# A four-layer perceiver in f32: norms tile by tile at the stage borders of its first layer, and small steps moved to GpSimd

## The chip, the cores and the metric

The kernel runs on one core of a Trainium2 chip. The metric is the device time in microseconds (us) of one execution, the median of the runs. A profile of one execution gives the trace from which all other durations are taken. The engines are named as in the profile: PE is TensorE's matmul, PEld its weight load, DVE is VectorE, ACT is ScalarE, POOL is GpSimd and SP is SyncE, which issues the DMAs. L12 is line 12 of the kernel.

## The reference

The network updates a residual stream x of 8 x 64 tokens by 256 channels. It reads a context of 1601 keys by 128 channels for each of the 8 batches. Each of its four layers has an attention into the context, a self-attention and a feed-forward part. The change touches the first layer, and a few bias rows and biases in the later ones. Its core is this (cut):

```python
def _mha(x, y, wq, wk, wv, li1_w, li1_b, lnx_g, lnx_b, lny_g, lny_b, ln3_g, ln3_b, li2_w, li2_b, li3_w, li3_b, causal):
    xn = _ln(x, lnx_g, lnx_b)
    yn = _ln(y, lny_g, lny_b)
    ...
    x_out = x + o @ li1_w + li1_b
    h = jax.nn.gelu(_ln(x_out, ln3_g, ln3_b) @ li2_w + li2_b, approximate=False)
    return x_out + h @ li3_w + li3_b
...
# xx is ln1(x); the second attention reads the context
# xx = ln2(xx + a1(xx, xx)); xx = a2(xx, context)
x = x + _L0_xattn_ref(_layernorm(x, axis=-1), ctx_512, ...)
x = x + _L0_attn_ref(_layernorm(x, axis=-1), ...)
x = x + _L0_ffn_ref(_layernorm(x, axis=-1), ...)
```

The comment lines put the body of the first attention block in words: a causal self-attention a1 with its own MLP, a norm with a gain and a bias (ln2), and a cross-attention a2 with its own MLP. b0 is the self-attention with rotated queries and keys that follows, and f0 the mixture of experts after it.

## The kernel before

The 512 tokens are held as four tiles (NI = 4) of 128 tokens by 256 channels in X, a tensor of 128 partitions x 4 x 256. The context has 13 tiles of keys (KT = 13). The stages run one after the other: a1, its MLP, a2, its MLP, b0, f0, and then three more layers (x1, r1, f1; x2, b2, f2; x3, b3, f3). Each engine works through its own queue in the order in which the kernel was scheduled, and pools of buffers decide when a tile may be written.

A norm of one tile (`normed_tile`, L324 to L333) takes five instructions. DVE computes the statistics (L328), the mean and variance (L330) and adds epsilon (L331). POOL raises the variance to the power of minus one half (L332, "the pow"). DVE subtracts the mean and multiplies (L333). `normed` does this for four tiles. `transposed` (L345) turns the normed tensor with PE through the identity (L352), and DVE copies the answer out with the gain and bias of the norm (L357), 512 columns at a time. `lin_T` (L363) then multiplies so that the channels lie on partitions ("psl" in the profile), and `lin_nat` (L373) so that the tokens do ("psn"); `lin_nat` hands each tile of its answer to a function `done`. `add_to` builds such a function: it adds the answer to one operand (L386) and then to further ones (L388) on DVE.

`after_attention` (L1092) is the MLP of a1 and of a2: norm, transposition, `lin_T` to 1024 channels with the gelu on ACT (L1101), `lin_nat` back to 256, where the answer and the row of biases are added to xo.

Four borders matter in what follows.

- Border 1, from a1 to its MLP: a1's answers are added to xo tile by tile (L1139). Then come the loads of the first two batches of the context ("cn"), its statistics on DVE (L1154, L1155), its scales on POOL (L1159 to L1162) and its normalisation on ACT (L1167). Only then is `after_attention` called.
- Border 2, from that MLP to a2: x1 += o over all four tiles at once (L1178), a norm, the gain (L1180) and bias (L1181) of ln2 over all tiles, a second norm, transposition, and `lin_T` for a2's queries ("psl_q" below is this `lin_T`).
- Border 3a, from a2's attention to its MLP: the last answer ("pso", L1223) is copied to qT, `lin_nat` projects it, and `add_to` adds x1 and a row, tile by tile.
- Border 3b, from that MLP to b0: x1 += o and X += x1 over all tiles (L1253, L1254). Then `small_attention` makes the turned biases ("shift", L1270 and L1271), and b0 starts with its norms, transposes (L411) and projections ("psq", "psk", L428).

```python
fetch(0)
fetch(1)
for k in range(0, KT, 3):
    stats(0, k)
scales(0)
for k in range(0, KT, 4):
    normalise(0, k)
```

`add_row_to_X` (L1089) adds a row of biases to all of X on DVE after four later stages, and b3 makes its own shift at L1273.

Of the kernel before, what the change touches and what calls it, by code (L numbers as in the profile page):

```python
# [11 lines left out]
F32 = mybir.dt.float32  # L12
# [5 lines left out]
P = 128  # L18
# [247 lines left out]
def perceiver(ctx: ExitStack, tc: tile.TileContext, d, col_at, row_at, const_at, out):  # L266
# [17 lines left out]
    ones = keep.tile([P, P], F32, tag="ones", name="ones")  # L284
    nc.gpsimd.memset(ones, 1.0)

    def K(name):
        n, w = const_at[name]
        return const[:, n : n + w]
# [32 lines left out]

    def normed_tile(dst, src):

        st = small.tile([P, 6], F32, tag="st", name="st")
        nc.vector.bn_stats(st, src)  # L328
        mv = small.tile([P, 4], F32, tag="mv", name="mv")
        nc.vector.bn_aggr(mv[:, 0:2], st)  # L330
        nc.vector.tensor_scalar(mv[:, 3:4], mv[:, 1:2], EPS, None, ALU.add)  # L331
        nc.gpsimd.tensor_tensor(mv[:, 2:3], mv[:, 3:4], mhalf[:, 0:1], ALU.pow)  # L332
        nc.vector.tensor_scalar(dst, src, mv[:, 0:1], mv[:, 2:3], ALU.subtract, ALU.mult)  # L333

    def normed(src, name="xn"):

        dst = nat.tile([P, NI, C], F32, tag="nat", name=name)
        for i in range(NI):
            normed_tile(dst[:, i, :], src[:, i, :])
        return dst  # L340

    def bc_rows(r):
        return r.unsqueeze(1).to_broadcast([P, NI, C])

    def transposed(ps, src, *affines):  # L345

        pairs = affines or (None,)
        dsts = [tpool.tile([P, C // P, NT], F32, tag="T", name="T") for _ in pairs]
        for c in range(C // P):
            t = ps.tile([P, 512], F32, tag="ps", name="pst")  # L350
            for i in range(NI):
                nc.tensor.transpose(t[:, i * P : (i + 1) * P], src[:, i, c * P : (c + 1) * P], ident)  # L352
            for dst, pair in zip(dsts, pairs):
                if pair is None:
                    evac(dst[:, c, :], t)
                else:
                    nc.vector.tensor_scalar(dst[:, c, :], t, col(pair[0], c), col(pair[1], c), ALU.mult, ALU.add)  # L357
        return dsts if affines else dsts[0]
# [727 lines left out]
        return done  # L1086

    def add_row_to_X(name):
        nc.vector.tensor_tensor(X, X, bc_rows(row(name)), ALU.add)  # L1089

    def general(n=8):
        return tc.tile_pool(name="ps", bufs=n, space=PSUM)  # L1092

    def after_attention(pre, xo, pool, ps):

        li2, li3 = chunks(weight(pre + "li2"), 1024), chunks(weight(pre + "li3"), C)
        [x3] = transposed(ps, normed(xo), (pre + "ln3_g", pre + "ln3_b"))
        hT = pool.tile([P, 8, NT], F32, tag="mlp", name="mlp")  # L1100
        lin_T(ps, li2, x3, 1024, lambda c, t: nc.scalar.activation(hT[:, c, :], t, AF.Gelu, bias=col(pre + "li2_b", c)))  # L1101
        r3 = row(pre + "li3_b")
        lin_nat(ps, li3, hT, add_to(xo, lambda i: xo[:, i, :], lambda i: r3))
        return xo

    with tc.tile_pool(name="l0res", bufs=1) as res, ExitStack() as both:
        x1 = res.tile([P, NI, C], F32, tag="x1", name="x1")
# [56 lines left out]
        def normalise(b, k):  # L1164
            mv, y = mvs[b], cns[b]
            for kt in range(k, min(k + 4, KT)):
                nc.scalar.activation(y[:, kt, :CY], y[:, kt, :CY], AF.Identity, bias=mv[:, kt, 3:4], scale=mv[:, kt, 2:3])  # L1167

        fetch(0)
        fetch(1)  # L1170
        for k in range(0, KT, 3):
            stats(0, k)
        scales(0)
        for k in range(0, KT, 4):
            normalise(0, k)
        with general() as ps, tc.tile_pool(name="m1", bufs=1) as mp:
            o = after_attention("a1", xo, mp, ps)
            nc.vector.tensor_tensor(x1, x1, o, ALU.add)  # L1178
            z = normed(x1)
            nc.vector.tensor_tensor(x1, z, bc_rows(row("ln2_g")), ALU.mult)  # L1180
            nc.vector.tensor_tensor(x1, x1, bc_rows(row("ln2_b")), ALU.add)  # L1181
        with tc.tile_pool(name="a2o", bufs=1) as op:

            qT = op.tile([P, 4, NT], F32, tag="qT", name="qT")
            with ExitStack() as _:
                wq, wk, wv, li1 = (weight("a2" + k) for k in ("wq", "wk", "wv", "li1"))
                wk3, wv3 = chunks(wk, CY), chunks(wv, P)
                with general() as ps:
                    [xT] = transposed(ps, normed(x1), ("a2lnx_g", "a2lnx_b"))
                    lin_T(ps, chunks(wq, 512), xT, 512, lambda c, t: evac(qT[:, c, :], t))  # L1190
                ps, psS, psO, fp = turned_pools("a2")
                with ps as ps, psS as psS, psO as psO, fp as fp:
                    cts, qks, oTs = {}, {}, {}
# [53 lines left out]
                    )  # L1247
                    turned_attention(ps, fp, *parts, hooks)
            with general() as ps, tc.tile_pool(name="m2", bufs=1) as mp:
                r1 = row("a2li1_b")  # L1250
                lin_nat(ps, chunks(li1, C), qT, add_to(xo, lambda i: x1[:, i, :], lambda i: r1))
                o = after_attention("a2", xo, mp, ps)
                nc.vector.tensor_tensor(x1, x1, o, ALU.add)  # L1253
                nc.vector.tensor_tensor(X, X, x1, ALU.add)  # L1254

    def small_attention(key, wq, wk, wvo, begin, xn, done, rope=None, bq=None, bk=None, bv=None):

        ps, psS, psO, pool = self_pools(key)  # L1260
        with ps as ps, psS as psS, psO as psO, pool as pool:
            shift = None
            if bq:
                shift = pool.tile([P, 4, P], F32, tag="shift", name="shift", bufs=1)
            for n, b in enumerate((bq, bk) if bq else ()):
                for c in range(2):
                    dst = shift[:, 2 * n + c, :]
                    if rope:
                        cs, sn = (x[:, c * P : (c + 1) * P] for x in rope)
                        nc.vector.tensor_scalar(dst, cs, col(b, c), None, ALU.mult)  # L1270
                        nc.vector.scalar_tensor_tensor(dst, sn, col(b + "s", c), dst, ALU.mult, ALU.add)  # L1271
                    else:
                        nc.vector.tensor_scalar(dst, ones, col(b, c), None, ALU.mult)  # L1273

            def project(i):
                [xT] = turned_tile(ps, pool, xn(i))
                if rope:
                    qk = rope_qk(ps, pool, xT, wq, wk, rope, shift)
                else:
                    t = ps.tile([P, 512], F32, tag="ps", name="psq")  # L1280
                    proj_tile(t[:, :C], wq, xT, 2)
                    proj_tile(t[:, C:], wk, xT, 2)
                    qk = pool.tile([P, 4, P], F32, tag="qkr", name="qkr")
                    nc.vector.tensor_tensor(qk, t.rearrange("p (c s) -> p c s", s=P), shift, ALU.add)
                return spread(pool, qk[:, 0:2, :], K("hm16"), 2), qk[:, 2:4, :], xT

            self_attention(ps, psS, psO, pool, begin, project, wvo[:, 0:2], wvo[:, 2:4], 16, done, bv=bv)
# [10 lines left out]
    def done0(i, t):  # L1298
# [7 lines left out]

    small_attention(
        "b0", (wq[:, 0:2], wq[:, 2:4]), (wk[:, 0:2], wk[:, 2:4]), wvo, begin0, lambda i: xn0[:, i, :], done0,
        rope=(K("r0c"), K("r0s")), bq="b0q", bk="b0k", bv="b0v",
    )  # L1310

    def attend_into_X(key, wq, wk, wvo, brow, **more):
# [350 lines left out]

    wqk, wvo = chunks(weight("b3qk"), C), chunks(weight("b3vo"), C)
    attend_into_X("b3", wqk[:, 0:2], wqk[:, 2:4], wvo, "b3d", bq="b3bq", bk="b3bk", bv="b3v")

# [45 lines left out]
```

## Time and profile before

| | before |
|---|---|
| median of 3 runs | 2319.57 us (2315.0 to 2322.26) |
| the profiled execution | 2313.45 us |
| its span | 2311.7 us |
| mean granted clock of TensorE | 0.951 |
| PE busy | 2068.4 us (89%) |
| PEld busy | 1430.7 us (62%) |
| DVE busy | 1321.3 us (57%) |
| ACT busy | 1003.3 us (43%) |
| POOL busy | 199.7 us (9%) |

The profiled execution's time is 1.75 us more than the span between its first and last record, and 6.1 us less than the median. In a line of the timeline, the first number is the start in us from the start of the span and the second the duration in us, then come the engine, the line, the operation, what it writes and reads, and how many instructions were put together; the bracket holds the idle time of the engine before it and what ended that. The granted clock is a share of full speed.

### The profile page before, as it was taken

The page shows a single profiled execution, that of the slowest core. Times are in us where ns is not written, and L with a number is a line of the kernel's source. Part 1 is how long each engine was busy: PE and PEld are TensorE (multiplying, and loading weights), DVE is VectorE, ACT ScalarE, POOL GpSimd, SP SyncE. Part 2 cuts the span into 40 slices and gives each one's busy share as a digit, 9 for nine tenths or more (in the row PEclk, how much of TensorE's full clock was granted, in tenths as well). Part 3 has the DMA queues.
Part 4 walks back from the last instruction along what each step waited for, and adds up shares of the span by engine and source line. Part 5 has one row for each costly group of instructions (what it writes and reads, how often), then busy time and mean ns, then how long its engine had stood idle before and what let it go on. Part 6 is the DMA issues. An engine that isn't in the chain of part 4 may idle for free. (4 is left out here: it accounts for less than half of the span.)

```text
span 2311.7 us, 35299 instructions
## 1 busy us (share of the span) xinstructions
PE 2068.4 (89%) x14916; PEld 1430.7 (62%) x14916; DVE 1321.3 (57%) x2171; ACT 1003.3 (43%) x1582; POOL 199.7 (9%) x258
## 2 busy tenths in 40 slices
PE   6678999999887998849999999999898899897988
PEld 5445777777675554538657777778554566565654
DVE  6346766666455223570266666675434788887533
ACT  2326766776312112301155556562114787774200
POOL 2101111110011000020000000001000111112000
PEclk9889999999988999959999999999799999999899
DMA  3210000000001225315400101001111000000010
GB/s 114 100 53 1 16 16 16 16 16 10 12 30 53 65 67 200 127 39 191 152 15 30 45 30 32 28 1 51 53 43 65 16 16 31 16 2 28 28 61 30
DMA packets 24941, 110.71 MB, mean 48 GB/s; under 512 B 3400, under 2 KB 6352, under 8 KB 21456
## 3 DMA queue, kind: packets, MB, share of 16 engines
q1 hardware_dynamic: 24784, 108.46, 13.5%
q8 instruction: 117, 1.92, 0.3%
q14 instruction: 40, 0.33, 0.0%
HBM read 107.93 MB, written 0.52 MB: 47 GB/s over the span
## 5 line engine op out<-in xcount | busy, mean ns | idle before, releaser
L837 PEld LDWEIGHTS psav<-cn,raw 128*128 128x128 f32 (+1 forms) x3328 | 402.9, 191 | 88.6 <-issue 87.3
L775 DVE TENSOR_TENSOR raw<-raw,mb 128x1024 f32<-128x1024 f32 (+1 forms) x336 | 384.0, 1147 | 84.5 <-ACT mb L771 84.5
L837 PE MATMUL psav<-cn,raw 128*128 128x129 f32 (+1 forms) x3328 | 407.0, 275 | 0.7 <-ACT raw L779 0.7
L825 PE MATMUL psS<-qk,ct 128*128 128x512 f32 (+1 forms) x832 | 397.7, 600 | 6.9 <-ACT raw L826 6.9
L753 DVE TENSOR_TENSOR top<-raw,top 128x1024 f32<-128x1024 f32 (+1 forms) x240 | 271.4, 1131 | 142.8 <-ACT raw L826 123.4
L779 ACT ACTIVATE raw<-raw 128x1024 f32<-128x1024 f32 (+1 forms) x336 | 335.4, 1001 | 15.9 <-DVE raw L775 14.9
L826 ACT COPY raw<-psS 128x512 f32<-128x512 f32 (+1 forms) x416 | 236.5, 587 | 126.4 <-PE psS L825 123.2
L825 PEld LDWEIGHTS psS<-qk,ct 128*128 128x128 f32 (+1 forms) x832 | 140.5, 187 | 129.2 <-issue 95.6
L332 POOL TENSOR_TENSOR mv<-mv,mhalf 128x1 f32<-128x1 f32 x76 | 41.6, 554 | 1130.4 <-DVE mv L331 1084.6
L1065 ACT ACTIVATE sg<-psg 128x512 f32<-128x512 f32 (+2 forms) x52 | 31.0, 596 | 244.5 <-PE psg L1062 244.4
L1066 DVE TENSOR_TENSOR hT<-sg,psu 128x512 f32<-128x512 f32 (+2 forms) x52 | 35.7, 687 | 145.4 <-PE psu L1062 145.4
L947 ACT COPY raw<-psS 128x1024 f32<-128x1024 f32 (+1 forms) x112 | 105.4, 941 | 2.0 <-PE psS L942 1.6
L942 PEld LDWEIGHTS psS<-qz,kT 32*128 32x128 f32 (+1 forms) x1664 | 54.8, 181 | 65.1 <-ACT raw L947 50.4
L747 DVE TENSOR_TENSOR top<-raw 128x1024 f32<-128x1024 f32 x48 | 58.8, 1226 | 58.8 <-ACT raw L826 36.8
L942 PE MATMUL psS<-qz,kT 32*128 32x128 f32 (+1 forms) x1664 | 76.9, 295 | 15.9 <-ACT raw L947 14.8
L963 PE MATMUL psav<-raw,v 128*32 128x128 f32 (+1 forms) x1664 | 86.7, 280 | 3.3 <-ACT raw L779 3.2
L1084 DVE SCALAR_TENSOR_TENSOR X<-psd,wt,X 128x256 f32<-128x256 f32 x128 | 58.5, 483 | 46.0 <-PE psd L1074 46.0
L963 PE MATMUL psav<-raw,ones 128*32 128x128 f32 (+1 forms) x1664 | 84.1, 274 | 0.0
L771 ACT COPY mb<-psmb 128x512 f32<-128x512 f32 x48 | 28.1, 586 | 124.9 <-PE psmb L769 124.9
L352 PE MATMUL pst<-const,xn 128*128 128x128 f32 x88 | 23.6, 384 | 54.4 <-DVE mv L331 27.7
L769 PE MATMUL psmb<-dg,ones 128*128 128x512 f32 x96 | 52.6, 630 | 13.1 <-DVE dg L763 13.0
L920 PE MATMUL psk<-ct,w_x3kv_None 128*128 128x401 f32 (+1 forms) x128 | 59.4, 550 | 0.7 <-ACT qT L319 0.7
(403 smaller groups left out, 3030.2 us busy)
## 6 DMA issues: line engine op xcount, KB each, us to landing
cn<-in_cn_dram SPq DMA_DIRECT2D x24, 838.5 KB, 4.6
ct<-in_ct_dram SPq DMA_DIRECT2D x24, 800.5 KB, 4.5
w_f1up<-in_f1up_dram SPq DMA_DIRECT2D x8, 1024.0 KB, 4.9
w_f1dn<-in_f1dn_dram SPq DMA_DIRECT2D x8, 1024.0 KB, 5.1
w_f2w<-in_f2w_dram SPq DMA_DIRECT2D x8, 768.0 KB, 4.3
w_f3w<-in_f3w_dram SPq DMA_DIRECT2D x16, 384.0 KB, 3.0
w_f0up<-in_f0up_dram SPq DMA_DIRECT2D x8, 704.0 KB, 4.0
w_f0dn<-in_f0dn_dram SPq DMA_DIRECT2D x8, 384.0 KB, 3.0
```

What stands on the lines that cost most here:

```text
L747: nc.vector.tensor_tensor(hd["top"], hd["raw", 0], raw, ALU.max)
L753: nc.vector.tensor_tensor(top[:n, :m, :], raw, top[:n, :m, :], ALU.max)
L775: nc.vector.tensor_tensor(raw, raw, halves[h]["mb"][:n].unsqueeze(1).to_broadcast([n, m, 512]), ALU.add)
L779: nc.scalar.activation(raw, raw, AF.Exp)
L825: nc.tensor.matmul(x[:n], ct[:, kt * P : kt * P + n], qk, start=True, stop=True)
L826: nc.scalar.copy(raw[:n, i, :], x[:n])
L837: nc.tensor.matmul(oa[:, j // 2, j % 2 * CO : (j % 2 + 1) * CO], w[:n, i, j * P : (j + 1) * P], cn[:n, kt, :], start=kt == 0 and j % 2 == ...
L920: nc.tensor.matmul(t[:, : hi - lo], wkv[:, c * P : (c + 1) * P], cts[b][:, lo:hi], start=True, stop=True)
L942: nc.tensor.matmul(x[:n, g, i * P : (i + 1) * P], kTs[h][r, kt * P : kt * P + n], qzs[b][r, c].rearrange("p m s -> p (m s)"), start=True, ...
L947: nc.scalar.copy(raw[:n, :m, :].rearrange("p i (g s) -> p i g s", g=4), x[:n, :, : m * P].rearrange("p g (i s) -> p i g s", s=P))
L963: nc.tensor.matmul(oa[r, at * P : (at + 1) * P], what, w[:n, i, g * P : (g + 1) * P], start=kt == 0 and at == 0, stop=kt == KT - 1 and at ...
L1084: nc.vector.scalar_tensor_tensor(X[:, i, :], t, w(i), X[:, i, :], ALU.mult, ALU.add)
```

## The change

At border 1 the norm, the transposition and the affine of each tile of xo are written as one step (`enter1` with `turn_into`), staggered by a tile against the statistics (`norm1`). A tensor `base` collects xo + x1 + the MLP's last bias row on POOL. The context's statistics, scales and normalisation, and the making of the turned biases of b0 (now on POOL, in a tensor `shift` that is kept for the whole kernel), move into `context_norm`. `after_attention` calls it between `lin_T` and `lin_nat`. At border 2, `leave1` handles each tile of the MLP's answer by itself: add, norm, gain, bias, norm, and the transposition of the tile two before it. At border 3a, POOL makes `x1r` = x1 + row and `base` = X + x1 + row, later + xo; `attended` adds and norms each tile, and the transposes run two tiles behind. At border 3b, X is the answer plus `base`, in one DVE step for each tile. `turn_into` copies the two halves of a transposed tile out by ACT and by DVE. `normed` issues the statistics of the next tile before the last step of a norm, and `transposed` goes by tiles ahead of columns. `add_row_to_X` and the shift of b3 move from DVE to POOL.

```diff
     def normed(src, name="xn"):
         dst = nat.tile([P, NI, C], F32, tag="nat", name=name)
-        for i in range(NI):
-            normed_tile(dst[:, i, :], src[:, i, :])
+        mvs = []
+        for i in range(NI + 1):
+            if i < NI:
+                mvs.append(norm_of(src[:, i, :]))
+            if i:
+                norm_by(dst[:, i - 1, :], src[:, i - 1, :], mvs[i - 1])
...
     def add_row_to_X(name):
-        nc.vector.tensor_tensor(X, X, bc_rows(row(name)), ALU.add)
+        nc.gpsimd.tensor_tensor(X, X, bc_rows(row(name)), ALU.add)
...
+    def turn_into(ps, dst, i, src, pair):
+        t = ps.tile([P, 512], F32, tag="ps", name="pst")
+        for c in range(C // P):
+            nc.tensor.transpose(t[:, c * P : (c + 1) * P], src[:, c * P : (c + 1) * P], ident)
+        for c in range(C // P):
+            d = dst[:, c, i * P : (i + 1) * P]
+            if c:
+                nc.vector.tensor_scalar(d, t[:, c * P : (c + 1) * P], col(pair[0], c), col(pair[1], c), ALU.mult, ALU.add)
+            else:
+                nc.scalar.activation(d, t[:, c * P : (c + 1) * P], AF.Identity, bias=col(pair[1], c), scale=col(pair[0], c))
...
-    def after_attention(pre, xo, pool, ps):
+    def after_attention(pre, xo, x3, pool, ps, done, meanwhile):
...
-        r3 = row(pre + "li3_b")
-        lin_nat(ps, li3, hT, add_to(xo, lambda i: xo[:, i, :], lambda i: r3))
-        return xo
+        meanwhile()
+        lin_nat(ps, li3, hT, done)
...
+        def context_norm():
+            for n, k in enumerate(("b0q", "b0k")):
+                for c in range(2):
+                    dst = shift[:, 2 * n + c, :]
+                    cs, sn = (K(x)[:, c * P : (c + 1) * P] for x in ("r0c", "r0s"))
+                    tmp = mp.tile([P, P], F32, tag="turned", name="turned", bufs=2)
+                    nc.gpsimd.tensor_scalar(tmp, sn, col(k + "s", c), None, ALU.mult)
+                    nc.gpsimd.tensor_scalar(dst, cs, col(k, c), None, ALU.mult)
+                    nc.gpsimd.tensor_tensor(dst, dst, tmp, ALU.add)
+            for k in range(0, KT, 3):
+                stats(0, k)
+            scales(0)
+            for k in range(0, KT, 4):
+                normalise(0, k)
...
+            def enter1(i):
+                norm_by(xn[:, i, :], xo[:, i, :], mvs1[i])
+                turn_into(ps, x3, i, xn[:, i, :], ("a1ln3_g", "a1ln3_b"))
+                nc.gpsimd.tensor_tensor(base[:, i, :], xo[:, i, :], x1[:, i, :], ALU.add)
+                nc.gpsimd.tensor_tensor(base[:, i, :], base[:, i, :], r3, ALU.add)
+
+            def leave1(i, t):
+                x = x1[:, i, :]
+                nc.vector.tensor_tensor(x, t, base[:, i, :], ALU.add)
+                normed_tile(z[:, i, :], x)
+                nc.vector.tensor_tensor(x, z[:, i, :], g2, ALU.mult)
+                nc.vector.tensor_tensor(x, x, b2, ALU.add)
+                normed_tile(xn[:, i, :], x)
+                turn2(i - 2)
...
+            staggered(norm1, enter1)
+            after_attention("a1", xo, x3, mp, ps, leave1, context_norm)
+            turn2(NI - 2)
+            turn2(NI - 1)
...
+                for i in range(NI):
+                    nc.gpsimd.tensor_tensor(x1r[:, i, :], x1[:, i, :], r1, ALU.add)
+                for i in range(NI):
+                    nc.gpsimd.tensor_tensor(base[:, i, :], X[:, i, :], x1[:, i, :], ALU.add)
+                    nc.gpsimd.tensor_tensor(base[:, i, :], base[:, i, :], r3, ALU.add)
+                def enter2(i):
+                    turn_into(ps, x3, i, xn[:, i, :], ("a2ln3_g", "a2ln3_b"))
+                    nc.gpsimd.tensor_tensor(base[:, i, :], base[:, i, :], xo[:, i, :], ALU.add)
+
+                def attended(i, t):
+                    nc.vector.tensor_tensor(xo[:, i, :], t, x1r[:, i, :], ALU.add)
+                    normed_tile(xn[:, i, :], xo[:, i, :])
+                    if i > 1:
+                        enter2(i - 2)
+
+                lin_nat(ps, chunks(li1, C), qT, attended)
+                enter2(NI - 2)
+                enter2(NI - 1)
+                after_attention(
+                    "a2", xo, x3, mp, ps, lambda i, t: nc.vector.tensor_tensor(X[:, i, :], t, base[:, i, :], ALU.add), lambda: None
+                )
...
+    for n, k in enumerate(("b3bq", "b3bk")):
+        for c in range(2):
+            nc.gpsimd.tensor_scalar(shift[:, 2 * n + c, :], ones, col(k, c), None, ALU.mult)
```

## The prediction, made before the changed kernel ran

> **What bounds the kernel now.** I read the page's busy line and slices first, then the table of windows around the four borders that the diff touches, then the timeline inside each border.
>
> ```profile
> PE 2068.4 (89%) x14916; PEld 1430.7 (62%) x14916; DVE 1321.3 (57%) x2171; ACT 1003.3 (43%) x1582; POOL 199.7 (9%) x258
> ```
>
> TensorE is busy for 89% of the span, so only its idle stretches can be won. They lie at the borders (columns: length, then busy us and count of PE, PEld, DVE, ACT, POOL, then the granted clock):
>
> ```profile
> 83.00:99.70 16.70, 2.56 (x8) 1.16 (x8) 7.79 (x44) 5.12 (x14) 5.42 (x8) 0.56 0.48 186
> 130.40:147.20 16.80, 2.57 (x9) 1.18 (x9) 13.50 (x45) 0.00 (x0) 4.34 (x8) 0.57 0.29 86
> 609.00:623.00 14.00, 9.28 (x57) 7.10 (x49) 8.78 (x27) 0.00 (x0) 2.41 (x4) 0.92 0.17 47
> 653.10:661.60 8.50, 0.00 (x0) 0.01 (x1) 7.96 (x24) 0.00 (x0) 2.83 (x11) 0.81 0.33 100
> 661.60:670.00 8.40, 7.88 (x38) 7.42 (x39) 3.12 (x7) 0.37 (x1) 5.25 (x8) 0.58 0.05 16
> ```
>
> PE idles 14.1, 14.2, 4.7 and 8.5 us in the first four, and the clock falls to about half. The timeline says what ends each wait:
>
> ```profile
> 87.11 0.49 DVE L1154 BATCH_NORM_STATS2 st<-cn 128x6 f32<-128x128 f32 x2 [4.36 <-DMA cn<-in_cn_dram]
> ...
> 94.49 0.56 POOL L332 TENSOR_TENSOR mv<-mv,mhalf 128x1 f32<-128x1 f32 x1
> ...
> 99.74 1.22 PE L369 MATMUL psl<-T,w_a1li_None 128*128 128x512 f32 x1 [0.69 <-DVE T L357]
> ```
>
> Border 1: DVE, in order, waits for the context's DMA, runs 13 tiles of its statistics, and only then normalises xo; POOL does the context's scales before the first pow (L332).
>
> ```profile
> 131.33 1.22 DVE L1178 TENSOR_TENSOR x<-x,xo 128x1024 f32<-128x1024 f32 x1
> ...
> 147.18 1.22 PE L369 MATMUL psl<-T,w_a2wq_None 128*128 128x512 f32 x1 [0.76 <-DVE T L357]
> ```
>
> Border 2 is a chain on DVE of whole-tensor steps (13.50 busy of 16.80).
>
> ```profile
> 613.73 0.57 POOL L332 TENSOR_TENSOR mv<-mv,mhalf 128x1 f32<-128x1 f32 x1 [107.68 <-DVE mv L331]
> ...
> 622.94 1.22 PE L369 MATMUL psl<-T,w_a2li_None 128*128 128x512 f32 x1 [0.69 <-DVE T L357]
> ```
>
> Border 3a is already staggered by tile: pow(0) runs while PE still works on the projection, and POOL is otherwise empty (107.68 us idle before it).
>
> ```profile
> 661.62 0.66 PE L411 MATMUL pst<-const,xn 128*128 128x128 f32 x2 [8.52 <-DVE mv L331]
> ```
>
> Border 3b: two 128x1024 adds and the turned biases ("shift") on DVE stand ahead of b0's first norm.
>
> **What the skill says.** "GPSIMD Engine Reference" (1. Specifications) says that GpSimd shares VectorE's port to SBUF and is held up while a VectorE instruction with two SBUF inputs runs, and gives a two-input elementwise step on it about twice VectorE's time. The trace agrees on the ratio: a 128x256 add is .727 us on POOL (L1125) against .42 on DVE (L386), 1.7 times. It also shows contention in one place and none in another:
>
> ```profile
> L1125 POOL TENSOR_TENSOR xo<-x,row_a1li_b x4: 726/727/728, 14.6 to 39.9; 128x256 f32<-128x256 f32 x4
> ```
>
> ```profile
> L972 POOL TENSOR_TENSOR res<-res,const x16: 460/1304/1362, 1810.5 to 2113.4; 128x128 f32<-128x128 f32 x16
> ```
>
> (min/median/max in ns: L972 is 2.8 times slower beside DVE's long two-input steps.) "TensorE: Matmul & The Clock Gate" (Part 1: The HAM clock gate) says that the clock halves after an idle window of some 3.4 us and takes about as long to return. Here a 128x512 matmul takes .855 us for about the first 5.5 us after 99.74 and .43 later, 3.1 us lost.
>
> **The change, part by part.** The program's instruction orders before and after show what stands behind what.
>
> *Border 1.* The context's loads, statistics and scales go behind xo's norms, which removes the 4.36 us wait, 13 x .26 us of statistics and the 3.5 us of scales from the path. But POOL's queue now holds six adds of 128x256 (base and bias rows, 6 x .727 = 4.36 us) ahead of the pow of tile 3, and their first waits for the last matmul of a1's projection, since base takes the room of a1's pool. So: xo(3) is ready at 82.35; adds to 86.7; pow .55 to 87.3; norm_by .41 to 87.75; two transposes, then evacuation by ACT and DVE in 128x128 pieces (.4), first psl at about 89.2 instead of 99.74: **-10.5**. PE idles from 83.2 to about 87.9, so the clock is still cold; nothing more is won. The four bias adds and turned-bias steps that follow end near 92.1 and the context's scales near 96.4; its 13 ACT normalisations then stand between gelus. The third gelu has its input at 97.1, so they should not delay it; a2 wants the context only after 147. Ends: -13.7 if pow(3) isn't held at all, -8 if the adds take 1.15 us.
>
> *Border 2.* Per tile, add, norm, two row steps and norm cost about 5.2 us of latency on DVE and POOL, and tiles overlap lin_nat, whose tile ends are 3.45 us apart. DVE's work for one tile is .42+1.5+.42+.42+1.5, about 4.3 us, more than 3.45, plus 3 to 4 pairs of the second context's statistics and the evacuations. Adding these up from the end of tile 0's matmuls gives psl_q 22.25 us later, against 120.05 to 147.18 (27.13) before: **-4.9** (-3 to -7). A wait is added here: the last psn matmuls stand behind the transposes of tile 0.
>
> *Border 3a.* L386's add, row add, norm and transposes stay per tile. What is new is POOL's queue: x1r (4 adds), X+x1 (4), +r3 (4), and base+=xo(0), **13 x .727 = 9.45 us, ahead of pow(0)**. The first waits for the last matmul of a2 (PE, 609.26), since x1r also takes freed room. So pow(0) starts at 618.8 to 619.4 instead of 613.73, and each next one stands behind another add and behind psn(3), which now follows the transposes of tile 0 on PE. Step by step norm_by(3) ends at 628.1 and psl starts at 629.2, against 622.94: **+6.3** (+3 to +10). PE's idle time is longer, so the cold start may cost part of the 3 us more.
>
> *Border 3b.* X = psn + base is one DVE step a tile, b0's norms of tiles 0 to 2 lie beside lin_nat, and shift was built some 500 us earlier. The first transpose needs only X(3): 653.1 + .5, and psq 1.16 later at 654.8, against 662.78: **-8.0**. PE idles 1.7 us instead of 9.7, so the clock stays up: groups of psq and psk took 2.08, 1.91, 1.91 and 1.34 us in the cold window against 1.06 warm, **-2.9**. Together **-10.9** (-8 to -13).
>
> *Small ones.* The row adds to X (1.23 us on DVE at 897.0, 1012.0, 1129.1, 1634.0) move to POOL (4 x .727 = 2.9 us there). Behind three of them DVE's evacuation of T gated PE by 1.17, 1.42 and 1.17 us; what is late next is the ACT half and PE's transposes, so I take .45, .6 and .45. b3's shift (1.41 us of DVE at 2118) goes earlier on POOL, ahead of b0's own later work there with over 7 us to spare: -1.6 with the pow that followed it. Sum **-3.1** (-5 to 0). The order of normed and transposed alone is worth 0: the transposes of before already run by tile (95.64, 96.70, 98.36). A moved row costs one more DMA issue on SP, with nothing urgent behind it. At the start of the program four constant steps enter POOL between the first pows; DVE waits there for a row until 13.5 us, some 5 us of slack: 0.
>
> Sum: -10.5 - 4.9 + 6.3 - 10.9 - 3.1 = **-23.1**. The profiled execution took 2313.45 us (span 2311.7), which gives 2290.4. It lies 6.1 below the median of 2319.57, and the same difference against the median is **2296**. About 0.3%, 7 us, is what a measurement of this kernel can tell from no change.
>
> **Rivals.**
>
> 1. *GpSimd's adds run at L972's contended rate, and it ends slower.* At 2.8 times, an add is 2.05 us. Border 3a's 13 adds cost 17 us more, border 1's six 8 more, and the context's scales come so late that ACT's in-order queue holds gelus back by some 12. Sum about +14, **2333**. It decides from about 1.55 us an add. For it: L972, and the skill's shared port. Against: L1125 stayed at .726 to .728 beside busy DVE, and DVE at 609 to 619 mostly waits or reads PSUM. Chance 0.07.
> 2. *POOL's adds cost the path nothing*, because they find their room free before the last matmul and are done by then. Border 1 gives -13.7, border 3a -2: sum about -35, **2285**. Against it: an engine's queue is in order, as L332 at 94.49 right behind L1162 shows. Chance 0.15.
> 3. *The borders shorten but the time is given back*: the clock stays cold at b0 (2.9 back), b0's own rope on POOL becomes the limit there (some 4), border 2's DVE chain wins only 2, border 3a costs 10. Sum about -10, **2309**. For it: POOL is busy 5.25 of 8.40 us at 661.6. Chance 0.15.
> 4. *It does less than it says*: the staggered norm changes nothing, as above; that is in the sum.
>
> The main case has the remaining 0.63. Faster by over 0.3%: main, rival 2 and most of rival 3, **0.87**; within: the weak end of rival 3, **0.06**; slower: rival 1, **0.07**. The main case alone spans 2284 to 2306 from the bounds above; with most of rivals 2 and 3 the range is 2281 to 2311.
>
> **What would show it.** Right: after a1, POOL runs six adds back to back right after the last psn, then a pow, and psl starts 6 to 7 us after xo(3); after a2, thirteen adds in a row of .73 us and psl 19 to 20 us after the last pso; at b0, PE idle for under 2 us with the clock over .9; psl_q some 1 to 2 us after the last evacuation, DVE nearly full before it. Wrong: adds over 1 us on POOL; pows that start during the adds; gelus waiting for ACT's normalisations; a cold clock at b0.

## The result, and the profile after

The changed kernel took 2286.03 us (median of 4 runs, 2284.82 to 2293.61), the kernel before 2317.28 us beside it. The ratio is 0.9874, with a 95% interval of 0.9851 to 0.9898: 29 us faster by the ratio. A second set of the same two kernels gave 2287.53 against 2318.64, again 0.9874 (0.9844 to 0.9904). The forecast was 2296, or 23.1 us less than before. The trace shown here is that of the slowest of the four runs (2293.61 us, span 2291.5), so its difference to the profiled execution before is only 19.8 us. Places are therefore compared stage by stage below, from mark to mark inside each trace.

The page's first line, and the windows of the four borders (columns as in the prediction):

```profile
PE 2070.3 (90%) x14916; PEld 1431.7 (62%) x14916; DVE 1308.9 (57%) x2152; ACT 1007.4 (44%) x1594; POOL 234.5 (10%) x302
```

```profile
82.80:89.70 6.90, 1.56 (x8) 0.93 (x8) 3.10 (x8) 1.61 (x4) 6.74 (x11) 0.89 0.84 313
...
120.40:132.20 11.80, 1.47 (x6) 0.59 (x6) 9.47 (x37) 1.37 (x3) 2.19 (x4) 0.73 0.37 111
...
592.70:611.00 18.30, 11.65 (x41) 8.68 (x41) 7.06 (x25) 1.87 (x5) 13.27 (x20) 0.80 0.16 43
...
640.20:641.70 1.50, 0.45 (x3) 0.20 (x2) 1.19 (x4) 0.37 (x1) 0.83 (x2) 1.00 0.48 71
641.70:650.30 8.60, 7.84 (x77) 7.22 (x77) 3.77 (x8) 2.57 (x5) 3.74 (x11) 1.00 0.24 87
```

PE's busy sum hardly moved (2068.4 to 2070.3 us, now 90%). POOL rose from 199.7 to 234.5. Three of the stretches without much PE are shorter than before, the third (border 3a) is longer: 18.3 us instead of 14.0 (and this window starts .4 us behind the mark of the table below), with POOL busy for 13.27 of it. At border 3b the clock stays at 1.00, and b0's first 8.6 us run at 1.00 instead of .58. From mark to mark:

| stretch (us) | before | after | difference | forecast |
|---|---|---|---|---|
| 1: end of a1's last psn to first psl | 17.46 | 6.97 | -10.5 | -10.5 |
| 2: end of last psn to a2's psl_q | 16.80 | 11.81 | -5.0 | -4.9 |
| 3a: last pso to first psl | 13.90 | 18.73 | +4.8 | +6.3 |
| 3b: end of last psn to first psq | 9.68 | 1.55 | -8.1 | -8.0 |
| b0: first psq to the end of its last psn | 54.65 | 54.53 | -0.1 | -2.9 |

**Border 1**, the timeline after:

```profile
82.96 1.44 POOL L1233 TENSOR_TENSOR base<-xo,x 128x256 f32<-128x256 f32 x2 [1.43 <-PE psn L568]
...
84.36 1.40 POOL L1234 TENSOR_TENSOR base<-base,row_a1li_b 128x256 f32<-128x256 f32 x2
85.72 1.40 POOL L1233 TENSOR_TENSOR base<-xo,x 128x256 f32<-128x256 f32 x2
87.08 0.55 POOL L335 TENSOR_TENSOR mv<-mv,mhalf 128x1 f32<-128x1 f32 x1
87.59 1.45 POOL L1234 TENSOR_TENSOR base<-base,row_a1li_b 128x256 f32<-128x256 f32 x2
87.66 0.80 DVE L339 TENSOR_SCALAR xn<-xo,mv 128x256 f32<-128x256 f32 x1 [2.23 <-POOL mv L335]
...
89.75 9.74 PE L384 MATMUL psl<-T,w_a1li_None 128*128 128x512 f32 x16 [0.55 <-ACT T L1121]
```

Six adds fill POOL from the end of the last projection until the pow of tile 3 at 87.08. The step that waited for them (L339) follows, and psl starts 2.1 us after its start. L339 takes .80 us here, beside two more adds on POOL (L1234); at the other borders the same step takes .41. All eight traces with these six adds have .80 or .81 for it.

**Border 2**: the last tile's chain on DVE.

```profile
124.01 0.42 DVE L1238 TENSOR_TENSOR x<-psn,base 128x256 f32<-128x256 f32 x1
...
130.05 0.41 DVE L339 TENSOR_SCALAR xn<-x,mv 128x256 f32<-128x256 f32 x1 [0.39 <-POOL mv L335]
...
132.20 8.99 PE L384 MATMUL psl<-T,w_a2wq_None 128*128 128x512 f32 x16 [0.99 <-DVE T L1119]
```

The last matmul ended at 120.39, but DVE reaches that tile only at 124.01, because the three tiles before it took up its queue for 14.2 us (5.2, 4.1 and 4.9). DVE was busy for 10.4 us of this; most of the rest is its wait for the pows on POOL.

**Border 3a**:

```profile
592.66 2.80 POOL L1325 TENSOR_TENSOR x1r<-x,row_a2li_b 128x256 f32<-128x256 f32 x4 [103.36 <-PE pso L1293]
...
600.88 0.72 POOL L1331 TENSOR_TENSOR base<-base,xo 128x256 f32<-128x256 f32 x1
...
601.56 0.58 POOL L335 TENSOR_TENSOR mv<-mv,mhalf 128x1 f32<-128x1 f32 x1
...
609.54 0.41 DVE L339 TENSOR_SCALAR xn<-xo,mv 128x256 f32<-128x256 f32 x1 [0.66 <-POOL mv L335]
...
611.00 14.54 PE L384 MATMUL psl<-T,w_a2li_None 128*128 128x512 f32 x30 [0.55 <-ACT T L1121]
```

POOL starts its adds with the end of the last pso and runs thirteen of them in 8.9 us, .685 apart, ahead of pow(0). Its adds show no contention; this is the answer on one line of them (min/median/max in ns):

```profile
L1328 POOL TENSOR_TENSOR base<-base,row_a2li_b x4: 721/724/727, 596.8 to 600.2; 128x256 f32<-128x256 f32 x4
```

**Border 3b**, and b0 some 19 us later:

```profile
640.25 0.42 DVE L1343 TENSOR_TENSOR X<-psn,base 128x256 f32<-128x256 f32 x1 [1.02 <-PE psn L393]
...
640.73 0.44 PE L426 MATMUL pst<-const,xn 128*128 128x128 f32 x2 [0.52 <-DVE X L1343]
...
641.76 1.16 PE L443 MATMUL psq<-xT,w_b0q_None 128*128 128x128 f32 x8 [0.59 <-ACT xT L431]
...
642.75 1.06 PE L443 MATMUL psw<-xT,w_b0q_None 128*128 128x128 f32 x8
...
660.67 2.02 PE L443 MATMUL psq<-xT,w_b0q_None 128*128 128x128 f32 x8
...
662.48 1.91 PE L443 MATMUL psw<-xT,w_b0q_None 128*128 128x128 f32 x8
```

The first groups of psq and psw take 1.16 and 1.06 us as forecast, but the half clock comes at the third tile instead (2.02 and 1.91 us for the same eight matmuls).

### The profile page after: what moved, and what is told of

Same layout as the page of the kernel before. It is cut to its first block, busy times and chain, and to the rows that moved or that the text cites. A ratio compares the mean times of both kernels' runs of the same rounds, so it can differ in the third digit from the quotient of the medians.

```text
span 2291.5 us, 35339 instructions
## 1 busy us (share of the span) xinstructions
PE 2070.3 (90%) x14916; PEld 1431.7 (62%) x14916; DVE 1308.9 (57%) x2152; ACT 1007.4 (44%) x1594; POOL 234.5 (10%) x302
## 3 DMA queue, kind: packets, MB, share of 16 engines
q1 hardware_dynamic: 24784, 108.46, 13.7%
## 5 line engine op out<-in xcount | busy, mean ns | idle before, releaser
L957 PE MATMUL psS<-qz,kT 32*128 32x128 f32 (+1 forms) x1664 | 77.4, 297 | 15.8 <-ACT raw L962 13.7
L945 PE MATMUL psv<-w_x3kv_None,ct 128*128 128x256 f32 (+1 forms) x208 | 56.8, 393 | 0.0
```

The costliest lines, as they stand in the source:

```text
L957: nc.tensor.matmul(x[:n, g, i * P : (i + 1) * P], kTs[h][r, kt * P : kt * P + n], qzs[b][r, c].rearrange("p m s -> p (m s)"), start=True, ...
```

## Experiments

All are edits of the changed kernel. Marks are compared within each trace; whole times move with the granted clock. Only old_order and all_early_again ran in the same rounds as the changed kernel. For the others the whole time is compared across rounds, in which the kernel before had medians of 2311.98 to 2320.14 us, so a few us of it decide nothing; most forecasts of whole times, reckoned from 2286, came out too low, by up to 9.5 us. Single runs of the kernel before ranged from 2306.63 to 2322.31 us on one chip, with mean clocks of .955 to .947.

**Border 3a without its adds (rows_early).** The sums with x1 are made in place while a2 runs.

```diff
+        rbo, rga = row("b0o"), row("gamma")
+        r1, r3 = row("a2li1_b"), row("a2li3_b")
+        for i in range(NI):
+            nc.gpsimd.tensor_tensor(X[:, i, :], X[:, i, :], r3, ALU.add)
+            nc.gpsimd.tensor_tensor(X[:, i, :], X[:, i, :], x1[:, i, :], ALU.add)
+            nc.gpsimd.tensor_tensor(x1[:, i, :], x1[:, i, :], r1, ALU.add)
...
-                for i in range(NI):
-                    nc.gpsimd.tensor_tensor(x1r[:, i, :], x1[:, i, :], r1, ALU.add)
-                for i in range(NI):
-                    nc.gpsimd.tensor_tensor(base[:, i, :], X[:, i, :], x1[:, i, :], ALU.add)
-                    nc.gpsimd.tensor_tensor(base[:, i, :], base[:, i, :], r3, ALU.add)
```

> Border 3a alone: X + r3 + x1 and x1 + r1 are made in place on POOL right after border 2, while a2 runs, instead of thirteen adds ahead of pow(0) after a2's last answer; only the add of xo stays. My account: pow(0) no longer waits, so the first psl of the second MLP comes 13 to 14 us after the start of the last answer's matmuls (pso) instead of 19.9, and the whole kernel is 6 us faster than the changed one (8 if the second MLP then starts with a warm clock): about 2279. Rival (the adds are hidden, and border 3a lost its time to psn(3) behind the transposes): the distance stays near 19.9 and the time near 2286.

Measured: 2288.25 us (ratio 0.9901, 0.9880 to 0.9922). Its timeline:

```profile
592.16 7.13 PE L393 MATMUL psn<-w_a2li_None,qT 128*128 128x256 f32 x24 [0.55 <-DVE qT L1302]
...
596.32 0.73 POOL L1341 TENSOR_TENSOR X<-X,xo 128x256 f32<-128x256 f32 x1 [107.90 <-DVE xo L1332]
...
597.18 0.58 POOL L335 TENSOR_TENSOR mv<-mv,mhalf 128x1 f32<-128x1 f32 x1
...
606.63 2.08 PE L384 MATMUL psl<-T,w_a2li_None 128*128 128x512 f32 x2 [0.55 <-ACT T L1121]
```

One add, then the pow, 5.8 us after the last pso instead of 9.3. From the last pso to psl it takes 15.24 us instead of 18.73, so 3.5 us of the border were POOL's queue. It isn't the 13 to 14 expected: the projection ran at half clock (24 matmuls in 7.13 us, where before 32 took 7.17). In the changed kernel this speed makes no difference: in eight traces with its thirteen adds pow(0) comes 9.26 to 9.29 us after the last pso, whether 24 matmuls take 7.13 us or 5.45, and the border takes 18.71 to 19.18 us. In all_early_again below, with the same edit as here, 24 of them took 5.45 us and the border 13.91 us, what it was before (13.90): then all that the border lost, 4.8 to 5.3 us, is POOL's queue. The place is settled by this. The gain in the whole time is not: 2279 us was expected, and 2288 us is no less than what the changed kernel takes.

**The slope of the same wait (adds_doubled).**

```diff
                 for i in range(NI):
                     nc.gpsimd.tensor_tensor(x1r[:, i, :], x1[:, i, :], r1, ALU.add)
+                for i in range(NI):
+                    nc.gpsimd.tensor_tensor(x1r[:, i, :], x1[:, i, :], r1, ALU.add)
                 for i in range(NI):
                     nc.gpsimd.tensor_tensor(base[:, i, :], X[:, i, :], x1[:, i, :], ALU.add)
+                    nc.gpsimd.tensor_tensor(base[:, i, :], X[:, i, :], x1[:, i, :], ALU.add)
```

> Border 3a's slope: x1r's four adds and the four adds X + x1 are each issued twice on POOL (the values are the same). My account: 7 to 8 more adds of .70 us stand ahead of pow(0), so the first psl comes 4.9 to 5.6 us later than in the changed kernel (about 25 us after the last pso) and the time rises by as much, to about 2291. Rival (adds hidden): no change, 2286. Rival (contention): adds of over 1 us, psl 8 us later or more.

Measured: 2295.39 us (0.9929, 0.9907 to 0.9951). The first adds on POOL, the pow behind them, what DVE does beside the next two adds, the next tile's pow, and psl:

```profile
594.90 2.79 POOL L1325 TENSOR_TENSOR x1r<-x,row_a2li_b 128x256 f32<-128x256 f32 x4 [103.37 <-PE pso L1293]
...
597.65 2.79 POOL L1327 TENSOR_TENSOR x1r<-x,row_a2li_b 128x256 f32<-128x256 f32 x4
...
608.56 0.58 POOL L335 TENSOR_TENSOR mv<-mv,mhalf 128x1 f32<-128x1 f32 x1
609.11 1.40 POOL L1334 TENSOR_TENSOR base<-base,xo 128x256 f32<-128x256 f32 x2
609.17 1.48 DVE L339 TENSOR_SCALAR xn<-xo,mv 128x256 f32<-128x256 f32 x1 [9.12 <-POOL mv L335]
...
611.48 0.56 POOL L335 TENSOR_TENSOR mv<-mv,mhalf 128x1 f32<-128x1 f32 x1 [0.97 <-DVE mv L334]
...
619.06 1.22 PE L384 MATMUL psl<-T,w_a2li_None 128*128 128x512 f32 x1 [0.55 <-ACT T L1121]
```

From the last pso to psl: 24.55 us, 5.8 more than in the changed kernel, where 4.9 to 5.6 was expected. Twenty adds in 13.7 us stand ahead of pow(0) instead of thirteen in 8.9, again .68 apart: that is 4.8 of the 5.8 us. Another .6 comes before the next tile's pow, and that one doesn't stand behind adds: POOL was idle for .97 us before it. It waited for DVE, whose L339 took 1.48 us instead of .41 beside two adds on POOL. The last .4 lies behind the third pow, where traces of the changed kernel differ by as much (18.73 and 19.17 us for the border). So the queue is the main cause. The adds themselves are not slowed (1.40 us for two), but a step of DVE beside them is.

**Border 1 without its adds (rows_inplace_1).** base becomes x1 itself, and shift is made on DVE at the start.

```diff
                 nc.gpsimd.tensor_tensor(xo[:, i, :], x, r1, ALU.add)
+                nc.gpsimd.tensor_tensor(x, x, r3, ALU.add)
...
-                nc.gpsimd.tensor_tensor(base[:, i, :], xo[:, i, :], x1[:, i, :], ALU.add)
-                nc.gpsimd.tensor_tensor(base[:, i, :], base[:, i, :], r3, ALU.add)
+                nc.gpsimd.tensor_tensor(x1[:, i, :], xo[:, i, :], x1[:, i, :], ALU.add)
...
-                nc.vector.tensor_tensor(x, t, base[:, i, :], ALU.add)
+                nc.vector.tensor_tensor(x, t, x, ALU.add)
```

> Border 1 alone: base is made in place in x1 (x1 + r3 during a1, then + xo as each tile of xo is ready), with no tile that must wait for a1's pool, and b0's turned biases are made on DVE at the start of the program. Then POOL holds at most one add of .70 us ahead of pow(3). My account: norm_by(3) ends near 85.2 on the scale of the changed kernel instead of 88.4, the first psl starts 3 us earlier (near 86.7), and PE's idle stretch of 4.4 us shrinks to 1.5 us, which may keep the clock up for up to 3 us more: 2280 to 2283. Rival (pow(3) was bound by DVE, the adds cost nothing): psl stays near 89.7 and the time near 2286.

Measured: 2287.80 us (0.9900, 0.9881 to 0.9919). The timeline at border 1:

```profile
83.57 0.73 POOL L1231 TENSOR_TENSOR x<-xo,x 128x256 f32<-128x256 f32 x1 [1.80 <-DVE xo L1173]
...
84.44 0.55 POOL L335 TENSOR_TENSOR mv<-mv,mhalf 128x1 f32<-128x1 f32 x1
...
85.59 0.40 DVE L339 TENSOR_SCALAR xn<-xo,mv 128x256 f32<-128x256 f32 x1
...
87.03 3.46 PE L384 MATMUL psl<-T,w_a1li_None 128*128 128x512 f32 x5 [0.55 <-ACT T L1121]
```

The pow of tile 3 runs at 84.44, one add ahead of it. From the end of a1 to psl it takes 4.00 us instead of 6.97: the 3 us that were expected. L339, at .40 us here instead of .80, is .4 of them. `lin_T`, timed to the first psn, is .9 us shorter too (15.54 against 16.44), but that isn't shown to come from this edit: in the eight traces with the changed kernel's border 1 it took 15.35 to 16.89. In this trace a2 took 2 us longer than in the changed kernel, and the whole time shows no gain where 3 to 6 us were expected.

**The context ahead of the norms (context_first).**

```diff
+            context_norm()
             staggered(norm1, enter1)
-            after_attention("a1", xo, x3, mp, ps, leave1, context_norm)
+            after_attention("a1", xo, x3, mp, ps, leave1, lambda: None)
```

> Border 1's main part undone: the context's statistics, scales and normalisation stand ahead of the norms of xo, as before; all else as in the changed kernel. My account: DVE waits for the DMA of the context until 87, then 3.5 us of statistics and POOL's scales; psl starts 9 to 10 us later than in the changed kernel, near 99, and the time is about 2295. Rival (the gain at border 1 comes from the staggered norms, not from the context): psl no more than 3 us later, 2289 at most.

Measured: 2304.47 us (0.9968, 0.9956 to 0.9980; 14 runs). Its timeline:

```profile
87.88 0.49 DVE L1187 BATCH_NORM_STATS2 st<-cn 128x6 f32<-128x128 f32 x2 [4.24 <-DMA cn<-in_cn_dram]
...
91.51 1.40 POOL L1234 TENSOR_TENSOR base<-base,row_a1li_b 128x256 f32<-128x256 f32 x2
...
93.00 0.28 POOL L1192 TENSOR_SCALAR cmv<-cmv 128x13 f32<-128x13 f32 x1
...
96.57 5.11 ACT L1200 ACTIVATE cn<-cn,cmv 128x128 f32<-128x128 f32 x13 [15.44 <-POOL cmv L1195]
...
101.58 1.48 ACT L1121 ACTIVATE T<-pst,cols 128x128 f32<-128x128 f32 x4
...
103.11 1.22 PE L384 MATMUL psl<-T,w_a1li_None 128*128 128x512 f32 x1 [2.59 <-ACT T L1121]
```

From a1's end to psl: 19.94 us, 13.0 more than in the changed kernel. With the staggered norms kept, the whole gain of border 1 is gone: it came from the move of the context's work, and the rival is out. It costs 3 to 4 us more than I expected, and the lines show two reasons. POOL is busy with shift and base until 92.9, so the context's scales start 1.3 us after its statistics, which end at 91.7. And the evacuations of T, half of them now on ACT, wait behind the 13 normalisations of the context in ACT's queue (96.57 to 101.7), while the transposes have been done since 100.5. On DVE alone, as before, they didn't have to.

**Border 2 with whole-tensor gain, bias and second norm (gain_bias_whole).**

```diff
-                normed_tile(z[:, i, :], x)
-                nc.vector.tensor_tensor(x, z[:, i, :], g2, ALU.mult)
-                nc.vector.tensor_tensor(x, x, b2, ALU.add)
-                normed_tile(xn[:, i, :], x)
-                turn2(i - 2)
...
+            for i in range(NI):
+                normed_tile(z[:, i, :], x1[:, i, :])
+            nc.vector.tensor_tensor(x1, z, bc_rows(g2), ALU.mult)
+            nc.vector.tensor_tensor(x1, x1, bc_rows(b2), ALU.add)
+            for i in range(NI):
+                normed_tile(xn[:, i, :], x1[:, i, :])
+            for i in range(NI):
+                turn2(i)
```

> Border 2, half undone: add and first norm stay tile by tile, but gain, bias and second norm run over all four tiles after the last one, and the transposes after that. If every tile-wise step pays (my sum), a2's first psl comes 4 us later than in the changed kernel. If DVE's own work of 4.9 us a tile, more than lin_nat's 3.45, is what bounds the tile-wise form, the whole-tensor steps (2 x 1.23 and 5.3 for the norms after 122.6) end near 130.4, as the tile-wise form does, and psl stays within 1 us of 132.2: 2286 in the latter case, 2290 in the former.

Measured: 2289.26 us (0.9877, 0.9851 to 0.9903). From the last psn to psl_q 11.97 us, against 11.81. The tile-wise gain, bias and second norm bring nothing that can be seen; the whole time, with its interval, could not tell the two cases apart. The last step of the first norm (the fourth tile's L333, now L339) shows where the 5 us come from, first in the kernel before, then in this one:

```profile
137.44 0.41 DVE L333 TENSOR_SCALAR xn<-x,mv 128x256 f32<-128x256 f32 x1 [0.73 <-POOL mv L332]
```

```profile
122.84 0.41 DVE L339 TENSOR_SCALAR xn<-x,mv 128x256 f32<-128x256 f32 x1 [0.66 <-POOL mv L335]
```

It ends 7.5 us after the last psn before and 2.4 us after it here: 5.1 us. From there to psl_q the two take 9.3 and 9.6 us. So the gain is in what this kernel keeps: the add and the first norm of three tiles beside `lin_nat`, and the bias row that left DVE.

**Border 3b with whole-tensor adds (x_adds_whole).**

```diff
-                    "a2", xo, x3, mp, ps, lambda i, t: nc.vector.tensor_tensor(X[:, i, :], t, base[:, i, :], ALU.add), lambda: None
+                    "a2", xo, x3, mp, ps, add_to(xo, lambda i: xo[:, i, :], lambda i: r3), lambda: None
                 )
+                nc.vector.tensor_tensor(x1, x1, xo, ALU.add)
+                nc.vector.tensor_tensor(X, X, x1, ALU.add)
```

> Border 3b, the adds undone: each tile's answer is added to xo and the row, then x1 += xo and X += x1 over all tiles, as before; the turned biases stay made ahead, and POOL's adds of border 3a still run. My account: b0's first transposes come 5.5 us later, and PE idles some 7 us, so b0's first projections run at half clock, 2.9 us more: 2291 to 2295. Rival (the gain at 3b came from the turned biases alone): within 2 us of 2286.

Measured: 2297.96 us (0.9912, 0.9883 to 0.9941). Its timeline, from the end of POOL's clearing of b0's tiles "vz":

```profile
648.29 0.27 POOL L460 MEMSET vz<- 64x8 f32 x2
648.64 0.55 POOL L335 TENSOR_TENSOR mv<-mv,mhalf 128x1 f32<-128x1 f32 x1
...
651.04 1.22 PE L443 MATMUL psq<-xT,w_b0q_None 128*128 128x128 f32 x4 [0.59 <-ACT xT L431]
```

From the last psn to psq 8.22 us against 1.55: 6.7 more, where 5.5 was expected. About 1 us of this is again POOL's queue: DVE had the first variance ready at 647.5, and its pow started at 648.64, behind the clearing. b0 takes 56.70 us, the longest of all traces. The sums made ahead are most of border 3b. The rest goes with the turned biases made ahead, which this kernel keeps: 1.5 us (9.68 before, 8.22 here), and more without that wait, as they took DVE 2.6 us before.

**The row adds on DVE again (rows_on_dve).**

```diff
-        nc.gpsimd.tensor_tensor(X, X, bc_rows(row(name)), ALU.add)
+        nc.vector.tensor_tensor(X, X, bc_rows(row(name)), ALU.add)
...
-            nc.gpsimd.tensor_scalar(shift[:, 2 * n + c, :], ones, col(k, c), None, ALU.mult)
+            nc.vector.tensor_scalar(shift[:, 2 * n + c, :], ones, col(k, c), None, ALU.mult)
```

> The small ones undone: the four row adds to X and b3's shift go back to DVE. My account: f1, x2 and f2 start .5 to 1 us later each and b3 1.6 later if the shift stands where it stood; together 2 to 3.5 us, 2288 to 2290. Rival (hidden): 2286.

Measured: 2290.76 us (0.9879, 0.9858 to 0.9900). The entry of f1, first in the changed kernel, then in this one:

```profile
993.54 2.35 POOL L1104 TENSOR_TENSOR X<-X,row_f1b 128x1024 f32<-128x1024 f32 x1 [0.53 <-DVE xn L339]
994.03 0.69 DVE L324 COPY T<-pst 128x512 f32<-128x512 f32 x1 [0.57 <-PE pst L366]
...
994.77 1.02 PE L1021 MATMUL psg<-w_f1g_None,T 128*128 128x8 f32 x4 [0.57 <-DVE T L324]
```

```profile
987.17 1.23 DVE L1104 TENSOR_TENSOR X<-X,row_f1b 128x1024 f32<-128x1024 f32 x1
...
988.31 0.68 DVE L324 COPY T<-pst 128x512 f32<-128x512 f32 x1
...
989.05 1.23 PE L1021 MATMUL psg<-w_f1g_None,T 128*128 128x8 f32 x5 [1.17 <-DVE T L324]
```

From the last pair of transposes to the gate's matmul (psg) it takes 1.86 us with the row on DVE and 1.26 without; at x2 1.86 and 1.18, at f2 1.86 and 1.33. That is 1.8 us in all, against 1.5 in the forecast. At b3 this kernel gains what was forecast for the changed one: from the end of x3's attention to b3's first psS it takes 12.12 us, against 13.71 before, with shift on DVE. What helps there is that shift is made long before b3 (at 676 to 688 us, during b0), in a tensor that is there from the start; that the engine matters can't be seen in these traces.

**The loops' order (old_order), and the changed kernel again (changed_again).** The first has the loops of `normed` (shown) and of `transposed` as before.

```diff
-        mvs = []
-        for i in range(NI + 1):
-            if i < NI:
-                mvs.append(norm_of(src[:, i, :]))
-            if i:
-                norm_by(dst[:, i - 1, :], src[:, i - 1, :], mvs[i - 1])
+        for i in range(NI):
+            normed_tile(dst[:, i, :], src[:, i, :])
```

> The changed kernel with the loops of the norm and of the transposition in the order of before (one tile's norm after the other; all tiles of a column, then the next column). My account: the built order of these instructions hardly differs, so 0, within 2 us of the changed kernel. Rival (the staggered norm is what makes f0, r1, f1, x2 and f2 start early): 3 us slower or more.

> The changed kernel once more, unaltered, beside the next two on one chip, because single executions of one kernel differ by up to 15 us with the granted clock. Expected ratio to before .986 to .989 (2285 to 2290 for 2316).

Measured in the same rounds: 2288.09 us and 2287.53 us, each 0.9874 of before. The entries of f1, x2 and f2 take 1.26, 1.18 and 1.33 us in both traces. The loops' order is worth nothing that these runs can tell.

**Both repairs together (all_early, all_early_again)**: the edits of rows_early and rows_inplace_1.

> Both repairs together (rows made in place during a2, base in place in x1, turned biases on DVE at the start). If the two waits behind POOL's adds are independent, their gains add: 6 at border 3a and 3 to 6 at border 1, so 2274 to 2277. If the clock gives it back later, 2280.

> The kernel with both repairs of POOL's queue, beside the changed one. Its trace showed the first two MLPs starting 1.5 and 5.2 us earlier than in the changed kernel, from a1's end that was 1.2 us later. If nothing takes this back, it is 5 to 7 us faster than the changed kernel in the same rounds; if the clock takes it back, within 2 us of it.

Measured: 2282.58 us (0.9845, 0.9823 to 0.9868), above the 2274 to 2277 expected, and 2279.23 us (0.9840, 0.9816 to 0.9864). In the second set the changed kernel had 2287.53, so this one was 8.3 us faster in the medians, a little more than expected. The intervals of the two ratios still overlap, while the single runs don't: 2277.69 to 2283.79 us, and 2284.24 to 2292.21. Where it gained is seen in the marks of both traces: 4.3 and 4.0 us from a1's end to psl instead of 6.97, and 15.06 and 13.91 from pso to psl instead of 18.73. It is the fastest version that was run.

## Why the prediction was right, point by point

- **Border 1** was right to a tenth (-10.5), and its mechanism too: context_first takes the gain away, rows_inplace_1 removes the six adds and finds the 3 us between my value and the bound of -13.7. What the sum left out is that L339 beside POOL's adds takes .80 us and not .41. It also read xo(3) as ready at 82.35, where the add only starts (82.32); that doesn't matter, as the adds on POOL wait for the last matmul (82.28 before), not for xo(3). PE's idle gap was 4.4 us, and `lin_T` still ran partly at half clock (16.44 us, against 16.66 before), as forecast; a cold start of it costs 2.8 us and not 3.1, as all_early_again, without half clock there, took 13.84. The half clock after this gap, in all eight traces with it, agrees with the Trainium skill's page "TensorE: Matmul & The Clock Gate" (Part 1: The HAM clock gate), which names an idle window of some 3.4 us. Below that figure of the page the traces differ among themselves, and a shorter gap was no safeguard: with 1.6 us of idle PE at border 1, two of three traces had 3.4 or 5.4 us of half clock in `lin_T` (rows_inplace_1, all_early) and one none (all_early_again). My reading that the clock falls to about half at four borders holds for the first two windows (.56, .57); the third and fourth show .92 and .81.
- **Border 2** was right in size (-5.0 for -4.9) and in the bound (tiles of 4.7 us on DVE in the mean, its waits included). The description as tile-wise steps hides that only their first part pays, as gain_bias_whole shows. One sign that I named did not come: psl_q started .05 us after the last copy out of the transposes, not 1 to 2.
- **Border 3a** had the right sign and cause; the term was oversized by 1.5 us. The thirteen adds were priced at .727 each, 9.45 us, and took 8.9, as adds back to back start .685 apart. The chain of pows behind them was priced too long as well: norm_by(3) ended 17.7 us after the last pso, where I had 19.1.
- **Border 3b** was right in its wait (-8.1 for -8.0). The clock term of -2.9 is the step that failed in this trace: the first tile's groups did run warm, but the half clock came 19 us later, where PE's longest idle stretch had been 1.4 us, and b0 took 54.53 us, against 54.65. In the eleven traces with the same border b0 took 50.2 to 54.6 us (51.1 in changed_again), and of the kernel before there is one trace only. So what a warm start is worth is not fixed by that start; I should have given it as 0 to 4.
- **The small ones** measured 1.8 us at f1, x2 and f2 (forecast 1.5), and 1.6 at b3 in rows_on_dve's trace. In the profiled execution b3's gain is covered by a projection at half clock just ahead of it (5.38 us instead of 3.69), and that mark reads 13.61; the wait just ahead of psS, behind the second pair of transposes, fell from 3.18 to 1.50 us.
- **The total** was 29 us, not 23.1. At the end of b0 the two traces of the changed kernel and that of old_order are 21.1, 21.3 and 21.1 us ahead of the kernel before, where the forecast's terms give 20.0. In the profiled execution that is in part luck: the 2.9 us that b0 did not win were made up by a2, 1.8 us shorter, and the second `lin_T`, about 1 us shorter, neither of which was forecast. Behind b0 the kernel before took 1594.2 us and the three traces 1595.2, 1589.2 and 1589.3, where the small ones explain 3.4. Between the two executions shown, this makes 19.8 us. The medians lie 31 us apart, as the profiled execution before was 3.8 us below the median beside it and the one after 7.6 us above its own.
- **The clock** moves these times, and its difference is not chance in a trace or two: the mean clock was .947 to .955 in the 31 runs of the kernel before that are on record with it, and .954 to .959 in the eight of the changed kernel. By the clock records of the traces, TensorE stood at half speed for 76 us until the end of b0 in the kernel before, and for 50 to 53 in these three; behind b0 for 150 us, and for 145 to 160. So the difference lies in the stages whose idle time the change shortens. How many of the 29 us come from it, beyond the waits themselves, stays open.
- **Rivals.** Contention on POOL is refuted for these stages: adds of .72 us throughout, 1.7 times DVE's .42, where the Trainium skill's page "GPSIMD Engine Reference" (4.1 Engine selection) has about twice. The page (1. Specifications) names contention between the two engines at SBUF; I read it as a hold-up of GpSimd. That did not come at border 3a, where DVE is busy for 7.06 of 18.3 us. What came was the reverse: DVE's L339 took .80 us instead of .41 beside POOL's adds at border 1, and 1.48 in adds_doubled. That POOL's adds cost nothing, rival 2, is refuted by adds_doubled and by border 3a, 4.8 us longer instead of 2 shorter. Its total of 2285 is nearer to the measured 2286 than mine, which shows that the whole time alone would have picked the wrong account. That the borders are given back by the clock happened in b0 in four of eleven traces (54.4 to 54.6 us), but not over the whole kernel; b0's own work on POOL did not become the limit at its start (3.74 of 8.60 us busy). That the staggered loops do nothing was right.

## What to carry to other kernels

Work that is moved to an empty engine is free only if nothing on the path stands behind it in that engine's queue: look for the small steps of the critical chain there (here one pow of .55 us), and ask from when the moved work can start at all. Sums that need no result of the current stage belong in the stage before, in place where possible, since a buffer that takes freed room starts only when that room is free. And time a border from mark to mark in the trace, since the clock moves the whole by as much as a border is worth.

## What was not expected of the hardware

- Two-input adds of 128x256 on POOL take .72 us each but start .685 us apart when they follow each other. A queue priced by single durations is some 6% too long.
- DVE's subtract-and-multiply of 128x256 in SBUF (L339) takes .41 us by itself, .80 beside POOL's adds (eight traces) and 1.48 beside two of them back to back (adds_doubled). The adds beside it take .72 to .79 us.
- One kernel's executions on one chip spread over 16 us (2306.63 to 2322.31), with the mean clock from .955 to .947. The half clock fell on different stages in two traces of the same kernel: b0 took 54.53 us in one and 51.12 in the other. In both, PE's longest idle stretch in b0's first 15 us was the same 1.4 us.
